# Turning the attention weights on VectorE and through memory, and one batch of weighted sums per pair of tiles

## The chip, the cores and the metric

The kernel runs on one core of a Trainium2 chip. A core has a matrix engine (TensorE, in the profile PE for its products and PEld for loading the stationary operand), a vector engine (VectorE, DVE), a scalar engine (ScalarE, ACT), GpSimd (POOL), and a queue engine (SyncE, SP) that issues transfers. Transfers are carried by 16 DMA engines. The on-chip memory SBUF has 128 partitions; products land in PSUM, which has eight banks of 128 x 512 fp32 values. The metric is the time of one execution on the device in microseconds (us), the median of several runs.

## The reference

Two layers over `x` of 128 graphs x 64 nodes x 768 features, with one adjacency matrix per graph. The first is a graph network with relation embeddings (pass 1 of the kernel), the second an attention layer with six heads of 128 features (pass 2). The change is in the second:

```
hh   = relu(layernorm(x))
h    = einsum('bni,hio->bhno', hh, W)              # six heads
th   = tanh(h);  attn = th@w_src + (th@w_dst)^T     # 64 x 64 per graph and head
attn = softmax(where(adj == 0, -999, leaky(attn)))
f    = elu(einsum('bhnm,bhmo->bhno', attn, h) + b)
gate = sigmoid(hh @ H_w.T + H_b)
out  = x + gate * f + (1 - gate) * hh
```

Everything is fp32.

## The kernel before

A tile is two graphs: 128 rows. There are 64 tiles in 32 pairs. Pass 1 (up to 1425 us) computes the first layer and leaves, per pair, three things in device memory: `x`, half of `hh`, and `hh` turned (`H1D`). Pass 2 reads them back pair by pair.

In pass 2 the products `hh @ [W | H_w]` of a pair are computed in a scheme with 15 products of thirds instead of 18 (`PRODUCTS`). Names in the written order are steps: `F<name>` forms a sum of operand blocks on VectorE (`form`); `P<k>.<q>` is one half of product k on TensorE (`half_product`, L1050); `R<k>` adds a product's bank to its place on VectorE (`read`, L1077, L1079), `RA<k>` the part that ScalarE copies where a place is begun (`read_act`, L1066). Products accumulate in four kinds of banks: `pma` (two buffers), `pmb`, `pmc`, `pmd` (one each), five of the eight banks. The other three are `ps`, taken in turn by everything else.

For each tile t of the pair (0 or 1) the attention follows: `th` tanh; `mul` multiply by the two vectors; `sum` row sums by ScalarE; `k`, `chain` small GpSimd work; `swap` a copy of the heads with the graphs exchanged (`hx`, two SP transfers, L1121); `rows`, `log` two small products; `rrow`, `lrow` their copies; `cp` the mask; `pre` leaky; `tr` row maxima; `exp` the exponentials into `pb` with their sums in `dn`; `rec` one over the sums. Then the weights are turned: `turnp` has three 128x128 transposes on TensorE into one `ps` bank (L1185), `pT` a ScalarE copy to SBUF (L1190). `att` computes the weighted sums (L1203): 12 products per tile, each with a stationary operand of 64 rows and 64 columns, so that four fit on the array side by side; the two row halves go to two `ps` banks. `ev` scales three heads by `dn` and adds the bias (L1213, VectorE), `e` exponentiates, `f` three final steps (L1231, L1233, L1235), `g` the gate, and `dma` adds the result to the output by a GpSimd transfer (L1238).

The order of all this is written out by hand as two strings. `ORDER` is one iteration of a loop over pairs; `name/k` means that the step is done for the pair k iterations back. `END` follows the loop and holds everything that is then left. Each engine executes its own instructions strictly in the order of these strings, except SP in pass 2, whose transfers are ordered by the planner; there the loads of the next pair are issued at an iteration's start. Six positions of iteration 0 (`j in (33, 56, ...)`) finish the last two tiles of pass 1. The queue's `load_h` (L369) fetches a pair's turned `hh` in eight transfers with pieces of 128 bytes.

Of the kernel before, what the change touches and what calls it, by code (L numbers as in the profile page):

```python
# [101 lines left out]


ORDER = """
R8/1 P7.0/1 f1.1/3 tr0/2 P9.0/1 P7.1/1 RA7/1 chain1/2 R7/1 P9.1/1 P11.1/1 f0.2/3 rows1/2 P10.0/1
R9/1 rrow1/2 exp0.0/2 P2.0 lrow1/2 P10.1/1 exp0.1/2 log1/2 P12.0/1 Ff1 turnp0/2 P12.1/1 f1.2/3
P0.0 R11/1 R10/1 th0/1 P13.0/1 P2.1 Ff8 cp1/2 mul0/1 Ff2 dma1/3 R12/1 Ff5 pre1/2 pT0/2 P0.1 Ff3
sum0.1/1 Ff7 P14.0/1 sum0.0/1 RA0 P13.1/1 memset0/1 Ff9 P14.1/1 R2 att0/2 sum0.2/1 tr1/2 Ff4
rec0/2 P5.0 R0 R13/1 dma0/3 Ff6 sum0.3/1 RA14/1 R14/1 exp1.0/2 ev0.1/2 k0/1 P3.0 chain0/1 Ff10
P1.0 exp1.1/2 th1/1 P3.1 ev0.0/2 turnp1/2 RA2 Ff11 e0/2 P1.1 P8.0 mul1/1 RA1 R1 P5.1 g1/1 pT1/2  # L110
rows0/1 R3 P4.0 lrow0/1 P6.0 f0.0/2 g0/1 att1/2 sum1.2/1 rec1/2 rrow0/1 f0.1/2 sum1.0/1 sum1.3/1
RA5 ev1.1/2 log0/1 swap1/1 sum1.1/1 swap0/1 P6.1 R5 ev1.0/2 e1/2 P4.1 P8.1 k1/1 R4 cp0/1 pre0/1
memset1/1 R6 P11.0 f1.0/2
""".split()

END = """
tr0/3 f0.2/4 R8/2 P7.0/2 P9.0/2 f1.1/4 P7.1/2 exp0.0/3 exp0.1/3 RA7/2 chain1/3 P9.1/2 memset0/2
P11.1/2 R7/2 rec0/3 R9/2 rows1/3 P10.0/2 Ff1/1 R11/2 th0/2 f1.2/4 turnp0/3 Ff2/1 P0.0/1 rrow1/3  # L120
P10.1/2 P12.0/2 pT0/3 lrow1/3 Ff3/1 log1/3 R10/2 dma0/4 Ff7/1 P0.1/1 g0/2 mul0/2 cp1/3 Ff8/1
P2.0/1 att0/3 P13.0/2 sum0.1/2 dma1/4 sum0.2/2 Ff4/1 R0/1 Ff5/1 P12.1/2 P13.1/2 Ff9/1 P2.1/1
RA0/1 sum0.0/2 ev0.1/3 ev0.0/3 P3.0/1 pre1/3 R13/2 sum0.3/2 tr1/3 Ff6/1 k0/2 P1.0/1 e0/3
exp1.0/3 chain0/2 P3.1/1 R12/2 P1.1/1 f0.0/3 RA1/1 rows0/2 P14.0/2 R2/1 RA2/1 R1/1 Ff10/1
rrow0/2 lrow0/2 P4.0/1 P14.1/2 exp1.1/3 log0/2 f0.1/3 R3/1 P5.0/1 Ff1 R14/2 f0.2/3 P6.0/1 cp0/2
P4.1/1 RA14/2 Ff11/1 turnp1/3 P6.1/1 th1/2 rec1/3 mul1/2 P5.1/1 pre0/2 pT1/3 R4/1 sum1.3/2
sum1.0/2 RA5/1 tr0/2 att1/3 P7.0/1 R5/1 Ff2 P8.0/1 ev1.1/3 P7.1/1 sum1.1/2 sum1.2/2 R6/1 Ff8
swap0/2 P9.0/1 k1/2 exp0.0/2 P11.0/1 Ff7 ev1.0/3 P9.1/1 chain1/2 swap1/2 g1/2 Ff5 P8.1/1 R7/1
P11.1/1 RA7/1 exp0.1/2 e1/3 Ff3 Ff4 rows1/2 P10.0/1 Ff6 R9/1 R8/1 R11/1 Ff9 lrow1/2 P12.0/1
th0/1 turnp0/2 rrow1/2 rec0/2 memset1/2 P10.1/1 f1.0/3 pT0/2 mul0/1 R10/1 PH2 sum0.3/1 log1/2  # L130
dma0/3 Ff10 P12.1/1 PH0 P13.0/1 R12/1 RAH2 sum0.0/1 P14.0/1 P13.1/1 att0/2 f1.1/3 sum0.2/1 cp1/2
pre1/2 f1.2/3 P14.1/1 tr1/2 sum0.1/1 R13/1 RAH0 ev0.0/2 PH3 PH1 exp1.0/2 PH5 R14/1 memset0/1
k0/1 ev0.1/2 chain0/1 rows0/1 RH3 Ff11 RA14/1 th1/1 e0/2 PH8 RAH1 exp1.1/2 mul1/1 PH4 rrow0/1
PH6 f0.0/2 swap0/1 lrow0/1 rec1/2 turnp1/2 sum1.1/1 sum1.0/1 sum1.3/1 RH4 pT1/2 memset1/1 log0/1
dma1/3 PH7 RH6 f0.1/2 cp0/1 RAH5 PH9 f0.2/2 PH11 RAH7 pre0/1 att1/2 RH9 g1/1 tr0/1 RH8 k1/1 PG0
RH11 sum1.2/1 ev1.0/2 PG5 g0/1 PH10 ev1.1/2 th0 chain1/1 PH12 RG0 mul0 RH10 rows1/1 rrow1/1
exp0.0/1 dma0/2 e1/2 PH13 exp0.1/1 sum0.1 f1.0/2 RH12 PG3 PG2 lrow1/1 log1/1 sum0.0 RH13 swap1/1
f1.1/2 sum0.2 PH14 rec0/1 PG1 RG2 sum0.3 cp1/1 turnp0/1 RG3 RAH14 pre1/1 f1.2/2 th1 RG1 tr1/1
PG6 k0 pT0/1 chain0 mul1 exp1.0/1 exp1.1/1 PG4 dma1/2 rows0 rrow0 RG4 att0/1 PG8 lrow0 ev0.0/1
turnp1/1 memset0 ev0.1/1 sum1.0 log0 PG7 memset1 pT1/1 RG6 rec1/1 e0/1 att1/1 sum1.2 RG5 PG9 cp0  # L140
sum1.1 sum1.3 pre0 f0.0/1 PG11 RG7 f0.1/1 k1 ev1.0/1 ev1.1/1 tr0 RG9 e1/1 chain1 exp0.0 rows1
f0.2/1 RG11 lrow1 rrow1 log1 swap1 exp0.1 f1.0/1 PG10 RG8 cp1 pre1 f1.1/1 tr1 turnp0 swap0 rec0
pT0 exp1.0 f1.2/1 att0 exp1.1 RG10 PG12 dma0/1 ev0.0 ev0.1 e0.0 rec1 RG12 f0.0.0 PG13 RG13
f0.1.0 e0.1 turnp1 PG14 g0 f0.0.1 RG14 f0.1.1 dma1/1 pT1 f0.2.0 att1 ev1.1 ev1.0 out0.0 f0.2.1
e1.1 f1.0.1 e1.0 g1 f1.0.0 f1.1.1 f1.1.0 f1.2.1 f1.2.0 out0.1 f1.3.1 f1.3.0 out1.1 out1.0
""".split()


# [1 line left out]
def kernel(  # L150
# [819 lines left out]
    with ExitStack() as px:  # L970
# [221 lines left out]
        def attend(t):


            hs = hz(t)[0]
            po = PO[t] = [pss.tile([P, 512], F32, name="ps")[:, : HH * DO].rearrange(
                "p (c o) -> p c o", c=HH) for r in range(2)]
            for c in range(HH):
                for g in range(GT):
                    for r in range(2):  # L1200
                        s = slice(r * N, (r + 1) * N)
                        o = slice(g * N, (g + 1) * N)
                        nc.tensor.matmul(po[r][o, c, :], PT[t][s, c, o],  # L1203
                                         (hs if r == g else HX[t])[s, 2 * c + r, :],
                                         start=True, stop=True)
# [206 lines left out]
```

## Time and profile before

| | us |
|---|---|
| median of 3 runs (lowest, highest) | 2384.75 (2384.31, 2386.83) |
| profiled execution | 2385.08 |
| its span | 2383.3 |
| pass 1 | to about 1425 |
| one period of pass 2 (one pair) | 29.18 |

| group of pass 2 | count | busy us |
|---|---|---|
| transposes of the weights, PE L1185 | 192 | 31.4 |
| copy of the turned weights, ACT L1190 | 64 | 30.4 |
| weighted sums, PE L1203 | 1536 | 112.7 |
| scaling of the sums, DVE L1213 | 384 | 110.1 |

The profile's busy times overlap on PE, since matmuls are pipelined: a group's sum is more than what it adds to the span. How far one instruction pushes the next is read from the distance between starts. A fp32 matmul appears as two records. Stretches of time are counted from the span's start.

### The profile page before, as it was taken

Reading aid. Unit: us, or ns where it says so; the run is one execution under the profiler, and the core shown is the slowest. Engines: PE = TensorE matmul, PEld = TensorE weight load, DVE = VectorE, ACT = ScalarE, POOL = GpSimd, SP = SyncE. Lnnn points to the kernel's source line nnn. Section 1 sums busy time; section 2 is a strip of 40 time slices with the busy share of each in tenths; the row PEclk is TensorE's granted clock in tenths of the full one; section 3 lists DMA queues with packets and bytes.
Section 4 is the critical chain, followed back from the end, with each engine's and each line's share of the span. In section 5 each row is a group of like instructions: output and inputs, shape, how many; then the busy total and the mean of one; then the engine's idle time right before and its main releaser. Section 6 shows DMA issues by size and latency. Waiting matters only on the chain.

```text
span 2383.3 us, 35466 instructions
## 1 busy us (share of the span) xinstructions
PE 2359.6 (99%) x11777; PEld 1660.7 (70%) x11777; DVE 1954.0 (82%) x3611; ACT 1339.6 (56%) x4017; POOL 381.6 (16%) x983
## 2 busy tenths in 40 slices
PE   9999999999999999999999999999999999999997
PEld 7888888888888888888888884444444444444445
DVE  8878787787787787877877876888888888888899
ACT  3454454544544544545545425677777777777777
POOL 1111111111111111111111111111111111111122
PEclk9999999999999999999999999999999999999999
DMA  5235335335344353353353466665555555555545
GB/s 186 83 89 139 101 94 151 90 98 142 89 117 123 89 136 104 92 151 92 96 143 89 108 187 125 117 113 109 109 110 114 115 113 110 109 109 114 114 94 100
DMA packets 582906, 271.80 MB, mean 114 GB/s; under 512 B 424394, under 2 KB 533053, under 8 KB 582722
## 3 DMA queue, kind: packets, MB, share of 16 engines
q1 hardware_dynamic: 572850, 244.71, 40.9%
q0 software_dynamic: 9728, 24.78, 7.0%
q8 instruction: 93, 1.52, 0.3%
q14 instruction: 91, 0.75, 0.1%
q10 hardware_dynamic: 144, 0.04, 0.0%
HBM read 119.66 MB, written 124.26 MB: 102 GB/s over the span
## 4 chain that ended last, share of the span: by engine, by line
PE 93%; DVE 3%; ACT 1%; DMA 1%; issue 0%; SPq 0%; POOL 0%; DVEq 0%; POOLq 0%; ACTq 0%
PE pwa L745 20%; PE pwb L745 17%; PE pwcd L745 13%; PE pma L1050 13%; PE pmb L1050 11%; PE pmc L1050 5%; PE pmd L1050 4%; PE pb L673 2%; PE ps L1203 2%; PE pwcd L729 1%; PE pwcd L673 1%; PE ps L1185 1%; ACT pr L1102 1%; PE ps L1154 1%; DVE weights L344 1%
## 5 line engine op out<-in xcount | busy, mean ns | idle before, releaser
L745 PE MATMUL pwa<-weights,op 128*128 128x256 f32 x2304 | 539.4, 381 | 0.3 <-DVE x L737 0.3
L745 PEld LDWEIGHTS pwa<-weights,op 128*128 128x128 f32 x2304 | 422.3, 190 | 53.8 <-issue 1.1
L745 PE MATMUL pwb<-weights,op 128*128 128x256 f32 x1932 | 454.5, 381 | 0.0
L745 PEld LDWEIGHTS pwb<-weights,op 128*128 128x128 f32 x1932 | 359.4, 190 | 53.1 <-issue 0.2
L344 DVE TENSOR_TENSOR op<-op 128x768 f32<-128x768 f32 x310 | 291.5, 949 | 95.6 <-ACT op L683 91.7
L745 PE MATMUL pwcd<-weights,op 128*128 128x256 f32 x1560 | 357.8, 379 | 0.0
L745 PEld LDWEIGHTS pwcd<-weights,op 128*128 128x128 f32 x1560 | 296.1, 190 | 40.1
L1050 PE MATMUL pma<-weights,op_f 128*128 128x512 f32 x620 | 310.3, 597 | 2.6 <-ACT hh L783 2.2
L683 ACT COPY op<-pb 128x512 f32<-128x512 f32 (+1 forms) x132 | 70.8, 618 | 320.5 <-PE pb L673 320.4
L1102 ACT ACTIVATE pr<-pr 128x128 f32<-128x128 f32 x768 | 225.3, 296 | 25.1 <-DVE pr L1092 25.0
L1050 PEld LDWEIGHTS pma<-weights,op_f 128*128 128x128 f32 x620 | 112.2, 190 | 140.4 <-issue 103.2
L1050 PE MATMUL pmb<-weights,op_f 128*128 128x512 f32 x372 | 193.1, 601 | 0.4 <-DVE hz L1077 0.4
L321 POOL TENSOR_SCALAR rn<-su 128x1 f32<-128x1 f32 x124 | 28.0, 226 | 902.0 <-ACT hf L316 531.1
L531 ACT ACTIVATE hp<-x,rn 128x768 f32<-128x768 f32 x60 | 107.7, 1796 | 109.8 <-POOL rn L323 109.8
L315 ACT ACTIVATE hf<-x 128x768 f32<-128x768 f32 x64 | 53.5, 836 | 163.6 <-DVE x L781 150.1
L1102 ACT ACTIVATION_READ_ACCUMULATOR pr<-pr 128x1 f32 x768 | 144.4, 188 | 0.0
L1175 ACT ACTIVATE pb<-al,mx 128x64 f32<-128x64 f32 x384 | 128.5, 338 | 12.3 <-DVE mx L1167 11.6
L1050 PE MATMUL pmc<-weights,op_f 128*128 128x512 f32 x248 | 129.7, 604 | 0.2 <-DVE weights L1079 0.2
L1213 DVE SCALAR_TENSOR_TENSOR f<-ps,dn,bb 128x128 f32<-128x128 f32 x384 | 110.1, 343 | 21.9 <-PE ps L1203 20.3
L1050 PE MATMUL pmb<-weights,h 128*128 128x512 f32 x248 | 127.7, 596 | 0.0
L737 DVE TENSOR_TENSOR x<-pwa,x 128x256 f32<-128x256 f32 x96 | 40.5, 422 | 100.0 <-PE pwa L729 72.1
L624 DVE TENSOR_REDUCE sum<-eq 128x26 f32<-128x1664 bf16 x64 | 120.0, 1875 | 0.1
...
## 6 DMA issues: line engine op xcount, KB each, us to landing
...
```

What stands on the lines that cost most here:

```text
L315: nc.scalar.activation(by, src, AF.Copy, scale=-1.0 / D, accum_out=sums[:, 0:1])
L344: return (nc.vector.tensor_add if s1 == "+" else nc.vector.tensor_sub)(to, x, y)
L531: nc.scalar.activation(hp.rearrange("p (b f i) -> p b f i", b=KB, f=NQ), X[t].rearrange("p (b i f) -> p b f i", b=KB, f=NQ), AF.Relu, scal ...
L624: nc.vector.tensor_reduce(SUM[p][:, k], EQ[p, k], AX.X, OP.add)
L673: nc.tensor.matmul(to[:, g, :, i, :], H0[2 * p + k][o, kb * P : (kb + 1) * P], rts[p % 2][o, k, :n].rearrange("p s n -> p (s n)"), start=T ...
L683: nc.scalar.copy(a[:, :n].rearrange("p s h (g n) -> p g (s h) n", g=GT), ps[:, :, c * n * KQ * N : (c + 1) * n * KQ * N].rearrange("p g (x ...
L745: nc.tensor.matmul(bank[b][:, :CQ], OPS[p, an][:, s, q, :], bw[bn][:, (s * KQ + q) * CQ : (s * KQ + q + 1) * CQ], start=(first and q == s ...
L1050: nc.tensor.matmul(bank[p, b], operand(p, an)[:, q, :], bw2[bn][:, 2 * q * CQ : 2 * (q + 1) * CQ], start=(first and q == 0), stop=(q == KQ ...
L1102: nc.scalar.activation(PR[t][:, j, h, :], PR[t][:, j, h, :], AF.Copy, accum_out=to)
L1175: nc.scalar.activation(PB[t][:, h, :], AL[t][:, h, :], AF.Exp, bias=MX[t][:, h : h + 1], accum_out=DN[t][:, h : h + 1])
L1203: nc.tensor.matmul(po[r][o, c, :], PT[t][s, c, o], (hs if r == g else HX[t])[s, 2 * c + r, :], start=True, stop=True)
L1213: nc.vector.scalar_tensor_tensor(FF[t][:, h * DO : (h + 1) * DO], PO[t][r][:, c, :], DN[t][:, h : h + 1], bb, op0=OP.mult, op1=OP.add)
```

## The change

- `turn_blocks` (`tv`): one VectorE transpose per tile that turns each 32x32 block of the 128x384 weights where it lies. `put_blocks` (`ts`): four SP transfers per tile write the blocks to device memory, in pieces of 128 bytes, each to where it belongs in the turned matrix. `get_blocks` (`tl`): one SP transfer reads the turned matrix back, in pieces of 512 bytes. They replace `turnp` and `pT` for all pairs but the last.
- `attend_both` (`att` without a tile number): the weighted sums of both tiles in one batch of 24 products over two `ps` banks and the banks `pmc` and `pmd`. In a bank each row half stays by itself. For the second last and the last pair `attend` per tile stays, for the last also `turnp` and `pT`.
- The load of `hh` for the final steps is a step of its own (`lx`), and so is the load of the next pair (`ld`). SP executes in written order too.
- `ORDER` and `END` are new throughout. Per tile, the steps `att`, `ev`, `e`, `f` are now up to four iterations behind. `FINISH` has the last two tiles of pass 1 finished in iterations 1 and 2.

```diff
+FINISH = (158, 189, 215, 216, 242, 268)
...
+    PTD = [dram.tile([KB // 2 * P, P], F32, name=f"pt_{t}") for t in range(NT)]
...
+        def turn_blocks(t):
+            TP[t] = work.tile([P, H * N], F32, name="tp")
+            nc.vector.transpose(TP[t], PB[t].rearrange("p h n -> p (h n)"))
+
+        def put_blocks(t):
+            for f in range(NQ):
+                nc.sync.dma_start(
+                    PTD[t].rearrange("(x i) (f n) -> f i x n", i=Q, n=Q)[f],
+                    TP[t][f * Q : (f + 1) * Q].rearrange("i (x n) -> i x n", n=Q))
+
+        def get_blocks(t):
+            PT[t] = work.tile([P, HH, P], F32, name="pT")
+            nc.sync.dma_start(PT[t], PTD[t].rearrange("(c p) n -> p c n", p=P))
+
+        def weigh(t, c, r):
+            hs = hz(t)[0]
+            s = slice(r * N, (r + 1) * N)
+            for g in range(GT):
+                o = slice(g * N, (g + 1) * N)
+                nc.tensor.matmul(PO[t][r][c][o, :], PT[t][s, c, o],
+                                 (hs if r == g else HX[t])[s, 2 * c + r, :],
+                                 start=True, stop=True)
...
+        def attend_both(p):
+            t = 2 * p
+            a, b, c, d = places(2, "cd")
+            PO[t] = a[:3], b[:3]
+            PO[t + 1] = (a[3], c[0], c[1]), (b[3], d[0], d[1])
+            for k in range(2):
+                for i in range(HH):
+                    weigh(t + k, i, 0)
+                    weigh(t + 1 - k, i, 1)
...
+            if n == "att":
+                attend_both(p)
+            elif n == "ld":
+                load(p + 1)
...
-        px.enter_context(tc.manual_schedule(engines=in_order))
+        px.enter_context(tc.manual_schedule(engines=in_order | {mybir.EngineType.SP}))
...
-            if i >= 0:
-                load(i + 1)
             for j, (n, k) in enumerate(order):
-                if i == 0 and j in (33, 56, 62, 78, 100, 106):
+                if i * len(order) + j in FINISH:
```

The new loop iteration, in which `att` is one batch:

```
dma0/4 R1/1 RA1/1 P3.1/1 R2/1 memset1/2 R14/2 th1/2 R3/1 tv1/3 P11.0/1 rows0/2 P4.0/1 rrow0/2
lrow0/2 tl0/3 mul1/2 P6.0/1 Ff1 P4.1/1 R4/1 Ff6/1 log0/2 P6.1/1 P11.1/1 sum1.2/2 R6/1 sum1.3/2
sum1.0/2 Ff7 sum1.1/2 P7.0/1 k1/2 cp0/2 Ff4 lx1/3 P7.1/1 rec0/3 Ff2 P9.0/1 Ff8 Ff11/1 R7/1 P9.1/1
pre0/2 RA7/1 tr0/2 chain1/2 P8.0/1 Ff9 P8.1/1 R9/1 lx0/3 rows1/2 Ff10 memset0/1 ld R11/1 g1/3
exp0.0/2 ts1/3 rrow1/2 R8/1 P10.0/1 P10.1/1 exp0.1/2 Ff3 swap0/3 lrow1/2 th0/1 P12.0/1 tv0/2 R10/1
P12.1/1 mul0/1 tl1/3 g0/2 att/3 log1/2 R12/1 ev1.0/3 ev1.1/3 cp1/2 sum0.3/1 ev0.0/3 sum0.1/1 P13.0/1
e1/3 f1.0/3 P13.1/1 P14.0/1 sum0.0/1 P14.1/1 P2.0 P2.1 R13/1 ev0.1/3 P1.0 pre1/2 f1.1/3 sum0.2/1
tr1/2 f1.2/3 P0.0 P0.1 e0/3 dma1/3 P5.0 f0.0/3 swap1/2 P5.1 exp1.0/2 RA0 R0 P1.1 exp1.1/2 f0.1/3
ts0/2 RA5 k0/1 chain0/1 rec1/2 Ff5 RA14/1 P3.0 f0.2/3 R5 RA2
```

More of the change, by code (lines that the diff above doesn't have):

```diff
@@ L104 @@
 ORDER = """
[L105 to L110, printed above, removed]
@@ L111 @@
-rows0/1 R3 P4.0 lrow0/1 P6.0 f0.0/2 g0/1 att1/2 sum1.2/1 rec1/2 rrow0/1 f0.1/2 sum1.0/1 sum1.3/1
-RA5 ev1.1/2 log0/1 swap1/1 sum1.1/1 swap0/1 P6.1 R5 ev1.0/2 e1/2 P4.1 P8.1 k1/1 R4 cp0/1 pre0/1
-memset1/1 R6 P11.0 f1.0/2
+dma0/4 R1/1 RA1/1 P3.1/1 R2/1 memset1/2 R14/2 th1/2 R3/1 tv1/3 P11.0/1 rows0/2 P4.0/1 rrow0/2
+lrow0/2 tl0/3 mul1/2 P6.0/1 Ff1 P4.1/1 R4/1 Ff6/1 log0/2 P6.1/1 P11.1/1 sum1.2/2 R6/1 sum1.3/2
+sum1.0/2 Ff7 sum1.1/2 P7.0/1 k1/2 cp0/2 Ff4 lx1/3 P7.1/1 rec0/3 Ff2 P9.0/1 Ff8 Ff11/1 R7/1 P9.1/1
@@ L114 @@
 """.split()
+FINISH = (158, 189, 215, 216, 242, 268)
 END = """
[L119 to L145, printed above, removed]
+Ff6/2 rows0/3 R1/2 P3.1/2 RA1/2 lrow0/3 tv1/4 Ff1/1 rrow0/3 R2/2 R14/3 P11.0/2 th1/3 P4.0/2
+memset1/3 R3/2 log0/3 ts1/4 tl1/4 Ff5/1 Ff11/2 mul1/3 P4.1/2 P6.0/2 P6.1/2 sum1.2/3 sum1.3/3 R4/2
@@ new lines @@
+lx1/4 P8.0/2 swap0/4 Ff7/1 sum1.0/3 P8.1/2 R6/2 sum1.1/3 P7.0/2 Ff2/1 k1/3 R8/2 P7.1/2 dma0/5 P9.0/2
+g1/4 Ff8/1 P9.1/2 cp0/3 Ff9/1 R7/2 Ff4/1 pre0/3 Ff3/1 P11.1/2 Ff10/1 RA7/2 lx0/4 tr0/3 R9/2 Ff6/1
+P10.0/2 chain1/3 rows1/3 R11/2 tl0/4 rrow1/3 th0/2 Ff11/1 P10.1/2 R10/2 g1/3 mul0/2 att/4 rec0/4
+lrow1/3 ev1.0/4 log1/3 ld/1 exp0.0/3 sum0.0/2 ev1.1/4 P13.0/2 P13.1/2 P12.0/2 sum0.1/2 ev0.1/4 cp1/3
+ev0.0/4 e1/4 R13/2 P12.1/2 exp0.1/3 P2.0/1 e0/4 k0/2 P2.1/1 f1.0/4 sum0.2/2 sum0.3/2 chain0/2 P0.0/1
@@ new lines @@
+R12/2 P0.1/1 f1.1/4 f0.0/4 f1.2/4 P1.0/1 f0.1/4 R0/1 tv0/3 P1.1/1 dma1/4 pre1/3 P5.0/1 g0/3 f0.2/4
+rows0/2 P14.0/2 P14.1/2 RA0/1 RA1/1 rec0/3 tr1/3 R2/1 R1/1 RA14/2 P3.0/1 lx1/3 P3.1/1 P5.1/1 P4.0/1
+R14/2 RA2/1 th1/2 R3/1 P4.1/1 memset0/2 exp1.0/3 rrow0/2 lrow0/2 P6.0/1 ts0/3 log0/2 mul1/2 P6.1/1
+exp1.1/3 swap1/3 R5/1 Ff1 P8.0/1 tv1/3 R4/1 Ff2 sum1.1/2 P7.0/1 cp0/2 R6/1 RA5/1 P7.1/1 sum1.0/2
+sum1.3/2 sum1.2/2 k1/2 P9.0/1 Ff5 Ff7 Ff8 Ff4 P9.1/1 RA7/1 rec1/3 pre0/2 P11.0/1 chain1/2 ts1/3 Ff9
@@ new lines @@
+swap0/3 tl0/3 lx0/3 tl1/3 Ff3 memset1/2 rows1/2 tr0/2 R7/1 dma0/4 Ff10 P11.1/1 lrow1/2 R9/1 P8.1/1
+Ff6 exp0.0/2 rrow1/2 R11/1 exp0.1/2 R8/1 th0/1 Ff11 log1/2 P10.0/1 cp1/2 P10.1/1 tv0/2 att/3 mul0/1
+pre1/2 sum0.0/1 R10/1 tr1/2 sum0.1/1 P12.0/1 P12.1/1 memset1/1 sum0.2/1 ev0.1/3 ev0.0/3 ev1.0/3 e0/3
+PG0 P13.0/1 swap1/2 ev1.1/3 memset0/1 g0/2 PH5 P13.1/1 f0.0/3 e1/3 R12/1 f0.1/3 exp1.0/2 PH2 R13/1
+f0.2/3 sum0.3/1 dma0/3 exp1.1/2 RAH2 f1.0/3 P14.0/1 g1/2 ts0/2 P14.1/1 R14/1 PH1 RA14/1 tv1/2 k0/1
@@ new lines @@
+tl0/2 RAH1 PH8 chain0/1 PH0 th1/1 f1.1/3 rows0/1 swap0/2 f1.2/3 PH4 mul1/1 RAH0 PH3 lx0/2 RAH5
+lrow0/1 sum1.1/1 sum1.0/1 sum1.3/1 PH11 RH3 ts1/2 PH6 lx0/1 rec1/2 rrow0/1 RH4 log0/1 RH6 PH7 k1/1
+RAH7 RG0 cp0/1 RH8 PH9 rec0/2 PH10 sum1.2/1 RH9 pre0/1 dma1/3 RH11 RH10 tr0/1 th0 PH12 exp0.0/1
+tl1/2 lx1/2 chain1/1 rows1/1 exp0.1/1 RH12 mul0 rrow1/1 sum0.2 tv0/1 att/2 sum0.0 ev1.1/2 PG3 sum0.1
+lrow1/1 PH13 PH14 ev0.1/2 ev0.0/2 RH13 log1/1 PG2 e0/2 ev1.0/2 RAH14 sum0.3 cp1/1 ts0/1 k0 pre1/1
+chain0 PG1 f0.0/2 rec0/1 e1/2 f0.1/2 rows0 memset0 RG2 th1 tr1/1 f0.2/2 exp1.0/1 mul1 exp1.1/1
@@ new lines @@
+swap0/1 g1/1 dma0/2 tv1/1 tl0/1 lrow0 RG1 RG3 ts1/1 rrow0 PG4 log0 PG6 sum1.2 sum1.0 att0/1 sum1.1
+f1.0/2 RG4 swap1/1 k1 sum1.3 f1.1/2 PG7 cp0 f1.2/2 chain1 ev0.0/1 tl1/1 ev0.1/1 RG7 rec1/1 pre0 tr0
+RG6 dma1/2 rows1 e0/1 PG5 f0.0/1 PG10 rrow1 g0/1 f0.1/1 exp0.0 lrow1 att1/1 PG9 swap1 RG5 log1
+memset1 f0.2/1 exp0.1 ev1.1/1 ev1.0/1 turnp0 PG8 RG10 cp1 lx1/1 e1/1 swap0 RG9 PG12 f1.0/1 pre1 tr1
+pT0 att0 exp1.0 f1.1/1 rec0 f1.2/1 dma0/1 PG11 lx0 RG12 ev0.1 dma1/1 ev0.0 PG13 RG8 PG14 exp1.1 RG13
@@ L146 @@
+e0.0 RG11 e0.1 f0.0.0 f0.0.1 rec1 lx1 RG14 f0.1.1 g0 turnp1 pT1 f0.1.0 g1 att1 f0.2.1 ev1.0 e1.0
+out0.1 ev1.1 f1.0.0 f1.1.0 e1.1 f1.0.1 f1.2.0 f1.1.1 f1.3.0 f1.2.1 f1.3.1 out1.0 f0.2.0 out0.0
+out1.1
 """.split()
@@ L1082, in hz @@
             return (hzs[t % NHZ][:, 0, :].rearrange("p (h o) -> p h o", h=H), hzs[t % NHZ][:, 1, :])
-        TH, PR, SD, SG, PS, AM, AL, PB, DN, MX, PT, PO, FF, EE, HX = ({} for _ in range(15))
+        TH, PR, SD, SG, PS, AM, AL, PB, DN, MX, PT, PO, FF, EE, HX, TP = ({} for _ in range(16))
         def tanh(t):
@@ new lines, in weigh, with places @@
+        def weigh(t, c, r):
[6 more added lines that the diff above has]
+                                 start=True, stop=True)
+        def places(n, more=""):
+            banks = [pss.tile([P, 512], F32, name="ps") for _ in range(n)]
+            banks += [psm.tile([P, 512], F32, name=f"pm{b}", bufs=1) for b in more]
+            return [[v[:, i * DO : (i + 1) * DO] for i in range(512 // DO)] for v in banks]
@@ L1192, in attend @@
         def attend(t):
-            hs = hz(t)[0]
-            po = PO[t] = [pss.tile([P, 512], F32, name="ps")[:, : HH * DO].rearrange(
-                "p (c o) -> p c o", c=HH) for r in range(2)]
+            PO[t] = places(2)
             for c in range(HH):
[L1199 to L1205, printed above, removed]
+                for r in range(2):
+                    weigh(t, c, r)
@@ L1213, in divide @@
                 nc.vector.scalar_tensor_tensor(
-                    FF[t][:, h * DO : (h + 1) * DO], PO[t][r][:, c, :], DN[t][:, h : h + 1], bb,
+                    FF[t][:, h * DO : (h + 1) * DO], PO[t][r][c], DN[t][:, h : h + 1], bb,
                     op0=OP.mult, op1=OP.add)
@@ L1242 @@
             "rrow": rows_dst, "lrow": rows_src, "memset": fill,
-            "log": lambda t: (load_x(t), logits(t)), "cp": choose, "pre": leaky, "tr": largest,
-            "rec": one_over, "turnp": turn_p, "pT": copy_p, "att": attend, "g": gate, "e": exp_f,
+            "lx": load_x, "log": logits, "cp": choose, "pre": leaky, "tr": largest,
+            "rec": one_over, "tv": turn_blocks, "ts": put_blocks, "tl": get_blocks, "turnp": turn_p, "pT": copy_p,
+            "att": attend, "g": gate, "e": exp_f,
             "dma": store,
@@ L1249, in step @@
         def step(n, p):
-            if n[0] == "F":
+            if n == "att":
+                attend_both(p)
+            elif n == "ld":
+                load(p + 1)
+            elif n[0] == "F":
                 form(p, n[1:])
@@ L1337, in last_step @@
                 step(n, p)
-                if n[:-1] == "log":
+                if n[:-1] == "lx":
                     load_out(2 * p + int(n[-1]))
@@ L1360 @@
                     step(n, i - k)
-        load(NP - 1)
         for n, k in parsed(END):
```

## The prediction, made before the changed kernel was run

> **What bounds the kernel now.** I read the engine totals first, then the busy time by stretch, then the chain of work that ended last, and last PE's order in time inside one period of pass 2. The totals:
>
> ```profile
> PE 2359.6 (99%) x11777; PEld 1660.7 (70%) x11777; DVE 1954.0 (82%) x3611; ACT 1339.6 (56%) x4017; POOL 381.6 (16%) x983
> ```
>
> PE is busy for all but 24 us. The stretches say where it is not (columns: stretch, length, busy time of PE, PEld, DVE, ACT, POOL, granted clock, DMA share, GB/s):
>
> ```profile
> 1429.00:1450.00 21.00, 18.76 (x44) 8.08 (x43) 11.27 (x20) 8.31 (x14) 2.26 (x10) 1.00 1.00 207
> ...
> 1878.28:1907.46 29.18, 29.18 (x119) 13.14 (x118) 26.19 (x55) 20.82 (x91) 5.11 (x17) 1.00 0.58 110
> ...
> 2286.80:2383.30 96.50, 81.28 (x457) 48.47 (x455) 88.15 (x191) 68.42 (x299) 21.37 (x55) 0.95 0.47 94
> ```
>
> The middle row is one period of pass 2: a pair of tiles each 29.18 us, PE without a gap, DVE idle for 3.0 us. The chain repeats at that distance 27 times (1478.27 to 2266.09 us). The last row is all that END writes out: there PE idles for 15 us and DVE for 8.35, so **END is set by VectorE**, the loop by PE. The chain in pass 2 agrees: its lines are the half products L1050 (80%), then L1203 (4.7%) and L1185 (1.9%).
>
> PE inside that period, start and length:
>
> ```profile
> 1885.42 1.02 PE L1050 MATMUL pma<-weights,op_f 128*128 128x512 f32 x2
> 1886.28 0.49 PE L1185 MATMUL ps<-ident,pb 128*128 128x128 f32 x3
> 1886.60 1.88 PE L1050 MATMUL pma<-weights,op_f 128*128 128x512 f32 x4
> ...
> 1892.62 1.02 PE L1050 MATMUL pma<-weights,op_f 128*128 128x512 f32 x2
> 1893.57 0.32 PE L1203 MATMUL ps<-hz,pT 64*64 64x128 f32 x1
> 1893.57 0.33 PE L1203 MATMUL ps<-hx,pT 64*64 64x128 f32 x2
> ...
> 1894.18 0.27 PE L1203 MATMUL ps<-hz,pT 64*64 64x128 f32 x1
> 1894.38 1.12 PE L1050 MATMUL pmc<-weights,op_f 128*128 128x512 f32 x2
> 1895.35 1.02 PE L1050 MATMUL pma<-weights,op_f 128*128 128x512 f32 x2
> ```
>
> Lengths overlap, so I price by start-to-start distance. A half product (two records) is 1886.28 - 1885.42 = 0.86, 0.858 over longer runs. Three transposes take 1886.60 - 1886.28 = 0.325. One tile's weighted sums take 1895.35 - 1892.62 - 2 x 0.858 = 1.01, the other tile's (ahead of a logit product) 0.91. Rows cost 0.083, logits 0.172. A period: 30 x 0.858 + 2 x (0.325 + 0.083 + 0.172) + 1.92 = 28.82. Most of the remaining 0.36 is P7 and P9 held up for VectorE's reads R4 and R6.
>
> **PE's part of the change.** The transposes go: -0.65 a pair. In the weighted sums four 64x64 quadrants start together, and then four every 0.107 us. Around a batch there are 0.10 us before it, 0.05 for the slower first step, and 0.10 + 0.11 before the wide products are back in step. Twelve steps in one batch cost 0.36 + 12 x 0.107 = 1.64 in place of 1.92: -0.28. The new period's work is 27.89.
>
> **VectorE's part.** One 32x32-block transpose of 128x384 is added per tile. The nearest row is pass 1's, the same instruction in f32 on twice the width:
>
> ```profile
> L793 DVE STREAM_TRANSPOSE ht<-hf x64: 916/969/978, 92.4 to 1439.6; 128x768 f32<-128x768 f32 x64
> ```
>
> Half is 0.49 us; two make DVE's period 26.19 + 0.98 = 27.17, against PE's 27.89. A rule speaks against this move: the Trainium skill, "VectorE: DVE Perf Modes", section "The three transpose paths", prices VectorE at 311 ns for 128x128 (bf16), and its rules for authors say to turn 128x128 on TensorE if PSUM will do. Three squares at that price are 0.93 a tile; DVE's period would be 28.05, and VectorE would set the loop. The row has the kernel's own type and form, so I take 0.49 and keep 0.93 for the range.
>
> **ScalarE** loses two copies of pT (L1190, 475 ns each). It is busy for 20.82 of 29.18; its share of the gain is nothing, since it sets no end in the loop.
>
> **New waits.** Writing each engine's steps of the new ORDER one after another with such distances (VectorE: form or half read 0.34, full read 0.60, multiply 1.66, final step 0.87, three divides 0.78, the 384-wide ones 0.43 to 0.48; stretched by 2%, as 25.68 before stood for 26.19 measured), PE reaches att at 14.9 and ends it at 16.5; its results are there at about 16.75. VectorE reaches ev1.0 at 16.0, so it waits there 0.75, and behind it stand ev1.1, cp1, ev0.0 and then e1 on ScalarE. That uses up its margin of 0.72 in one place. What PE needs from VectorE is then still early: R3 done at 1.8 for P6 at 2.7, R4 at 5.3 for P7 at 6.3, f11 at 8.6 for P8 at 9.7. Banks c and d, which att borrows, are read (R11, R8) by 12.3, and ev1.1 frees them at 18.3 for P2 at 20.1. So paper gives no stall; I take 0.25 a period (nothing to 0.7), since margins of one us are met by an in-order VectorE with 0.7 to spare.
>
> **SP and the queues.** Per pair SP now issues 8 puts of 48 KB and 2 gets of 192 KB more: 25 transfers in place of 15, at 0.3 to 0.55 each some 11 of 27.9 us. SP is in written order now: swap1 waits for att, ts0 stands behind it, tl0 waits for ts0's landing, and behind tl0 stand both x loads and all of the next pair's loads (needed 20 us later). The tight one is tile 1: tv1 ends at 2.1, its four puts are issued by 4.0, then swap0 (5.1), then tl1. In pass 1 such a put and reload is visible:
>
> ```profile
> 1273.75 0.36 SPq L542 DMA_DIRECT2D h<-hpt  x1
> 1276.33 0.36 SPq L556 DMA_DIRECT2D op<-h  x1
> ```
>
> 2.6 us from put to reload. The load of the next pair (6,144 packets of 128 B) lies ahead. Over ten periods 71,230 packets took 39.8% of 16 engines over 291.8 us, 26 ns each, so it drains in at most 10 us and, begun near -4, by about 5; puts until 8, landed 9, tl1 landed 12; att wants it at 14.9. Three us are left. The puts add 3,072 packets of 128 B and the gets 768 of 512 B a pair: at 26 ns, 6.2 us of the 16 engines. DMA goes from 0.58 x 29.18 = 17.0 to 23.2 us of 28.1, a share of 0.83.
> The Trainium skill, "DMA: Bandwidth & Descriptors", Specifications, speaks against the puts: under 512 B a transfer is a read-modify-write. The row is for reads in 128 B pieces; 128 B writes to DRAM are not in this trace. Nothing is lost up to (28.1 - 17.0 - 1.2) x 16 / 3,072 = 51 ns a packet; there the queue is full. By the row the sum is the forecast; past 51 ns it is the third rival.
>
> **The sum.** Pass 2 before: iteration 0 holds 17 half products (14.6), iteration 1 26.0, 28 periods of 29.18 are 817.0, and PE's waits at its beginning 2.9 (L1050 for ScalarE L783, 2.2): 860.5, from 1426.0 to END at 2286.8. The new order runs a longer pipeline: iteration 0 holds 9 half products (7.7), iteration 1 25.7, iteration 2 26.3, then 27 periods of 28.14 are 759.8; beginning 1.5, because the last tiles of pass 1 are finished an iteration later: 821.0. **END therefore gets longer.** By the distances above its list held 85.0 us of VectorE before (88.15 measured, x1.037) and holds 100.2 now: 103.9, and with the same 8.35 idle 112.3 in place of 96.5. Span: 1426.0 + 821.0 + 112.3 = 2359.3, against 2383.3. The profiled execution took 2385.08, 1.8 more than its span, and the median is 2384.75; so 2361. Of 40 us that the loop gives, END takes 16 back. END from 106 (better order) to 119, stalls from 0 to 0.7: 2348 to 2379, with both ends at once unlikely: 2350 to 2373.
>
> **Rivals.** (1) PE's rate holds, as above: chance 0.65, including a luckier end down to 2345. (2) *VectorE becomes the loop's bound*: 28.05 by the page's price plus 0.3 of waits; 27 x 28.35 = 765.5, END +3.4: about 2370; up to 2380 with more waits. For it: only 0.7 of margin, against 3.0 before. Chance 0.18. (3) *The reload is late*, at att, on PE: a wait takes the place of the transposes. The gain is used up when tl1 lands more than 24/27 = 0.9 us past 14.9 in every period beyond my 0.25; two us late give 2361 + 54 = 2415, one us 2388. Three us of margin and a DMA share under 0.9 are against it. Chance 0.08. (4) *The batch doesn't do what it says*: the new order issues both quadrants of one row half before the other's; if only two run together, 24 steps of 0.107 make it 2.93, the period 29.4, and the time 2361 + 27 x 1.29 + 4 = 2400. That the trace starts all four within 0.02 us speaks against it. Chance 0.04. The rest, 0.05, is stalls that nearly cancel the gain.
>
> A measurement tells about 0.2% (5 us) from no change. Faster: (1), (2) and 0.03 of the near-cancelling stalls, 0.86. Same: their other 0.02 and the mildest 0.02 of (3), 0.04. Slower: the rest of (3), and (4), 0.10. For 8 in 10 I go from 2345 to 2378.
>
> **What would show it.** Marks of the period 28.0 to 28.3 apart; no L1185 in the loop; one batch of 48 matmul records of about 1.5 us; L1205 at 0.5 us; DVE 96% busy in the loop; END near 2247, about 112 long, VectorE over 90% busy. Wrong if PE waits at the sums for a DMA, if DVE is at 100%, or if END isn't longer.

## The result, and the profile after

The changed kernel takes 2364.59 us (median of 4 runs, 2362.86 to 2365.44), the kernel before on the same chip 2385.52 (4 runs). The ratio is 0.9911, 95% interval 0.9894 to 0.9928: 0.9% faster. The forecast of 2361 is 3.6 us too low. The profiled execution took 2364.23 us with a span of 2362.4.

Line numbers have moved: the half products (L1050 before) are L1059, the weighted sums L1224, the scaling of the sums L1260, the three final steps L1278, L1280 and L1282, split L1122 and L1124, SP's `h` loads L378.

The engine totals of the changed kernel's page:

```profile
PE 2326.6 (98%) x11591; PEld 1654.4 (70%) x11591; DVE 1979.1 (84%) x3673; ACT 1303.9 (55%) x3955; POOL 441.4 (19%) x983
```

PE has 33 us less, VectorE 25 more, and GpSimd 60 us more with the same 983 instructions. That last number was in no step of the forecast; the part of it that falls in END (32.2 us where END had 21.4 before) bears on what the forecast missed.

The busy time by stretch (stretch, length, busy PE, PEld, DVE, ACT, POOL, granted clock, DMA share, GB/s): one period, what END writes out, and the loop ahead of it.

```profile
1753.62:1781.50 27.88, 27.88 (x113) 12.83 (x113) 26.99 (x57) 19.64 (x90) 6.75 (x16) 1.00 0.71 145
2238.74:2362.40 123.66, 93.44 (x506) 55.13 (x505) 101.81 (x222) 75.30 (x325) 32.17 (x60) 0.87 0.61 130
1426.00:2238.74 812.74, 812.74 (x3166) 372.80 (x3167) 768.40 (x1590) 562.40 (x2507) 198.92 (x474) 1.00 0.70 141
```

A period is 27.88 us where it was 29.18. VectorE is busy for 97% of it, and PE still has no gap. The loop ends 8.3 us earlier than forecast (812.7 us, not 821.0). END is 11.4 us longer than forecast (123.7, not 112.3), and PE works at a mean clock of 0.87 there. So the total was close because two errors cancel, and in part by luck: a loop that was better than I said, and an END that was worse.

The loop has no transposes of the weights on PE left: the six that remain (L1194) are those of the last pair, in END. The batch begins like this in time (start, length, instruction); the four quadrants start within 0.03 us of each other, and a new set follows every 0.11 us:

```profile
1751.81 0.32 PE L1224 MATMUL ps<-weights,pT 64*64 64x128 f32 x1
1751.81 0.33 PE L1224 MATMUL ps<-hx,pT 64*64 64x128 f32 x2
1751.83 0.41 PE L1224 MATMUL ps<-weights,pT 64*64 64x128 f32 x2
...
1753.28 0.34 PE L1163 MATMUL ps<-rrow,lrow 82*128 82x384 bf16 x1
```

From the batch's first start to the logit product behind it are 1.47 us. The VectorE transposes as a group (shortest, median and longest ns, first and last start, shape):

```profile
L1205 DVE STREAM_TRANSPOSE tp<-pb x62: 560/564/575, 1472.6 to 2321.2; 128x384 f32<-128x384 f32 x62
```

Lengths overlap: behind the one that starts at 2264.08 the next instruction starts at 2264.58, 0.50 us later (forecast 0.49).

**END.** VectorE did less work there than forecast (101.8, not 103.9) but idled for 21.9 us, not 8.35. Of that, 7.4 us lie behind its last instruction, and the longest gaps before instructions are these (in brackets the idle time ahead, and who ended it):

```profile
2270.05 0.42 DVE L1086 TENSOR_TENSOR hz<-pma,weights 128x256 f32<-128x256 f32 x1 [3.38 <-ACT hz L1075]
2303.85 0.42 DVE L1339 TENSOR_TENSOR weights<-weights,pma 128x256 f32<-128x256 f32 x1 [4.07 <-PE pma L1322]
2343.40 1.64 DVE L1260 SCALAR_TENSOR_TENSOR f<-ps,dn,bb 128x128 f32<-128x128 f32 x6 [2.93 <-DMA out_dram<-f]
```

The first one can be followed back. PE, in time:

```profile
2262.43 1.02 PE L1059 MATMUL pmc<-weights,op_f 128*128 128x512 f32 x2
2265.89 0.38 PE L1144 MATMUL ps<-idr,sdb 128*82 128x192 bf16 x1 [2.44 <-POOL sdb L1122]
2266.07 5.25 PE L1059 MATMUL pma<-weights,op_f 128*128 128x512 f32 x8
```

PE waits 2.44 us for `rows`, that is for GpSimd's small `chain` (split, L1122 and L1124). Eight half-bank records then take 5.1 us from start to start, where they take 3.4 elsewhere: after the wait the granted clock was 0.52 for 3.4 us, by the busy times of that stretch:

```profile
2265.80:2269.20 3.40, 3.31 (x5) 1.58 (x6) 0.87 (x3) 0.00 (x0) 1.35 (x3) 0.52 0.82 105
```

The Trainium skill, "TensorE: Matmul & The Clock Gate", Part 1, says that TensorE falls back to 4 of 8 clock pulses after an idle window of about 3.4 us and is released after about 3.4 us of busy time. The 0.52 and the 3.4 us of this stretch fit; the wait was shorter than that window, and a second execution (below) had the same wait without the slow clock. In this execution the wait of 2.44 us thus cost some 1.6 us more. GpSimd's instructions in that time:

```profile
2261.14 2.75 POOL L1122 CAST sdb<-sg 128x18 bf16<-128x18 f32 x1 [4.23 <-issue]
...
2264.25 0.20 POOL L1122 CAST sdb<-sg 128x18 bf16<-128x18 f32 x1
2264.53 1.05 POOL L1124 TENSOR_TENSOR sg<-sg,sdb 128x18 f32<-128x18 f32 x1
```

VectorE's, in the same time:

```profile
2261.14 0.95 DVE L1278 SCALAR_TENSOR_TENSOR f<-e,f 128x768 f32<-128x768 f32 x1
2262.01 0.94 DVE L1282 SCALAR_TENSOR_TENSOR f<-weights,f 128x768 f32<-128x768 f32 x1
2262.88 0.95 DVE L1280 SCALAR_TENSOR_TENSOR f<-f,x 128x768 f32<-128x768 f32 x1
2263.75 0.41 DVE L1086 TENSOR_TENSOR weights<-pma,weights 128x256 f32<-128x256 f32 x1
```

A cast of 18 columns takes 0.20 us, or 2.75 us where VectorE runs three final steps in a row, whose operands are all in SBUF; it ends when VectorE goes on to an operand in PSUM. It starts right behind ScalarE's last sum for this tile, which ends at 2261.0. The chain of work that ended last runs through it (start, length, what; "issue" is time for which the profile shows no cause):

```profile
2256.91 4.22 issue
2261.14 2.76 POOL sdb L1122
2264.53 1.05 POOL sg L1124
...
2266.28 5.04 PE pma L1059 x8
```

Added up over END, split's two lines take 11.2 us of that chain, and 1.1 us of the chain in END before. Some 38 of its 118 us are "issue", so the chain alone doesn't settle what holds END.

### The profile page after: what moved, and what is told of

The parts are those of the page before. It is cut to its first block, busy times and chain, and to the rows that moved or that the text cites. A ratio compares the mean times of both kernels' runs of the same rounds, so it can differ in the third digit from the quotient of the medians.

```text
span 2362.4 us, 35548 instructions
## 1 busy us (share of the span) xinstructions
PE 2326.6 (98%) x11591; PEld 1654.4 (70%) x11591; DVE 1979.1 (84%) x3673; ACT 1303.9 (55%) x3955; POOL 441.4 (19%) x983
## 4 chain that ended last, share of the span: by engine, by line
PE 93%; DVE 3%; issue 2%; DMA 1%; POOL 1%; ACT 0%; SPq 0%; POOLq 0%; DVEq 0%
PE pwa L754 21%; PE pwb L754 17%; PE pwcd L754 14%; PE pma L1059 13%; PE pmb L1059 11%; PE pmd L1059 4%; PE pmc L1059 4%; PE pb L682 3%; PE ps L1224 1%; PE pwcd L738 1%; PE pwcd L682 1%; PE ps L1163 1%; DVE weights L353 1%; PE pmc L1224 0%; PE pwa L738 0%
## 5 line engine op out<-in xcount | busy, mean ns | idle before, releaser
L1059 PE MATMUL pma<-weights,op_f 128*128 128x512 f32 x620 | 293.1, 595 | 0.0
L1059 PEld LDWEIGHTS pma<-weights,op_f 128*128 128x128 f32 x620 | 118.2, 191 | 147.6 <-issue 139.2
L1059 PE MATMUL pmb<-weights,op_f 128*128 128x512 f32 x372 | 180.7, 594 | 0.0
L1285 POOL DMA_DIRECT2D out_dram<-f x62 | 55.0, 886 | 390.1 <-DVE f L1282 376.8
L1059 PEld LDWEIGHTS pmb<-weights,op_f 128*128 128x128 f32 x372 | 68.4, 190 | 83.7 <-issue 76.0
L1059 PE MATMUL pmb<-weights,h 128*128 128x512 f32 x248 | 122.5, 595 | 0.0
L1059 PE MATMUL pmc<-weights,op_f 128*128 128x512 f32 x248 | 121.8, 592 | 0.0
```

Source lines behind the costliest of these rows:

```text
L1059: nc.tensor.matmul(bank[p, b], operand(p, an)[:, q, :], bw2[bn][:, 2 * q * CQ : 2 * (q + 1) * CQ], start=(first and q == 0), stop=(q == KQ ...
L1285: nc.gpsimd.dma_start(of[t * P : (t + 1) * P, :], FF[t], accum_op=OP.add)
```

## The experiments

The theories: (A) in the loop PE's own work sets the time, and the change gains by taking work off PE; in END PE waits for GpSimd's chain, and VectorE waits for PE. (B), the prediction's: END is set by the amount of VectorE's work. Rivals for the loop: VectorE at 97% is as good as the bound; the reload is close to the path.

### One part undone at a time

*split_batch* cuts the batch in two, each part with one row half of either tile, and puts the logit product between them; *turn_on_pe* puts the three TensorE transposes and ScalarE's copy back, and keeps the batch; *both_back* does both. The new order is kept in all three.

```diff
-P12.1/1 mul0/1 tl1/3 g0/2 att/3 log1/2 R12/1 ...
+P12.1/1 mul0/1 tl1/3 g0/2 atA/3 log1/2 atB/3 R12/1 ...
```

```diff
-dma0/4 R1/1 RA1/1 P3.1/1 ... R3/1 tv1/3 P11.0/1 rows0/2 P4.0/1 rrow0/2
-lrow0/2 tl0/3 mul1/2 P6.0/1 ...          (and no ts, tl, tv elsewhere)
+dma0/4 R1/1 RA1/1 P3.1/1 ... R3/1 turnp1/3 P11.0/1 pT1/3 rows0/2 P4.0/1 rrow0/2
+lrow0/2 turnp0/3 mul1/2 pT0/3 P6.0/1 ...
```

> In the loop the batch of weighted sums is cut in two, with the logit product of the other tile between the halves; nothing else changes (END keeps its batches). If the entry and exit of a batch cost PE what was read off the trace before (0.28 us a period), the period goes from 27.88 to about 28.16 us and the time to 2364.6 + 27 x 0.28 = 2372. If the batching is worth nothing, because VectorE or a transfer sets the period, the period stays at 27.9 and the time at 2365. If the cut leaves a stall behind ev1.0, more than 28.3 and above 2376.

> The changed kernel's order, with the weights turned by three TensorE transposes and a ScalarE copy again in place of the VectorE transpose, the puts and the reload; the batch stays. If PE sets the loop, the period grows by two times three transposes, 0.65 us, to 28.53, and the time is 2364.6 + 27 x 0.65 = 2382, less up to 4 us in END, where VectorE has 0.5 us less for each of the last seven tiles: 2378 to 2382. If VectorE or the reload set the loop, taking their work away leaves the period at 27.9 or below, and the time at 2365 or below.

> Both parts undone in the changed order: transposes on TensorE, batch cut in two. If they add up, the period is 27.88 + 0.65 + 0.28 = 28.81 us, the 0.37 left to the 29.18 of before is what the new order saves in stalls, and the time is about 2388: above the kernel before, since END stays longer than before's. If the order alone carries the gain, the time stays near 2365.

Measured (single executions; the kernel before took 2386.7 beside them): 2373.64, 2383.08 and 2393.71 us. The busy times of one period, for split_batch:

```profile
1752.55:1780.79 28.24, 28.24 (x114) 12.85 (x113) 27.17 (x57) 19.64 (x88) 6.73 (x16) 1.00 0.69 137
```

for turn_on_pe:

```profile
1755.39:1783.94 28.55, 28.55 (x119) 13.41 (x119) 26.39 (x55) 20.50 (x91) 6.96 (x16) 1.00 0.56 114
```

and for both_back:

```profile
1758.53:1787.43 28.90, 28.90 (x120) 13.41 (x119) 26.50 (x55) 20.50 (x91) 6.89 (x16) 1.00 0.58 112
```

Against 27.88 the batch is worth 0.36 us a period, the transposes 0.66, both together 1.01: they add. (The expectations had 0.28, 0.65 and 0.93.) What is left of the 1.30 between before and after, 29.18 - 28.90 = 0.28, belongs to the new order alone, which has both old parts and still stalls less. That order by itself is no gain: both_back is slower than before (2393.7 against 2386.7). Its loop ends 20 us earlier than the old one (at 2266.8), but its END is 125.2 us long where it was 96.5; the 2388 that was expected of it is 6 us too low.

### VectorE loaded to the brim

*turn_twice* does each VectorE transpose twice.

```diff
-            nc.vector.transpose(TP[t], PB[t].rearrange("p h n -> p (h n)"))
+            for _ in range(2):
+                nc.vector.transpose(TP[t], PB[t].rearrange("p h n -> p (h n)"))
```

> Each VectorE transpose of the weights is done twice (same output); nothing else changes. VectorE is busy for 26.98 of 27.88 us in a period; two more transposes bring its work to about 27.98. If PE sets the period with VectorE 0.9 below it, the period goes only to 28.0 to 28.3, and END grows by some 4 us: 2371 to 2380. If VectorE sets the period already, the whole 1.0 us is added: 28.9, and 2395.

Measured (a single execution, beside 2386.7 of the kernel before): 2362.02 us. The busy times of one period and of END:

```profile
1750.00:1777.88 27.88, 27.88 (x114) 12.83 (x113) 27.78 (x59) 19.66 (x89) 6.79 (x16) 1.00 0.71 144
2239.60:2360.20 120.60, 90.24 (x505) 52.93 (x505) 105.62 (x229) 75.31 (x325) 29.70 (x62) 0.91 0.63 134
```

VectorE is busy for 99.6% of a period and the period doesn't move, not even by the 0.1 to 0.4 us that my own theory expected, whose 2371 to 2380 us were wrong too. END has 3.8 us more VectorE work and is 3 us shorter (1 us, against the second execution below). Both the rival for the loop and theory B fall here: VectorE's work in END isn't what sets its length.

### The puts doubled

*puts_twice* issues each of a pair's eight puts twice, to the same place.

```diff
-            for f in range(NQ):
+            for f in (*range(NQ), *range(NQ)):
```

> Each of the eight puts of a pair (48 KB in pieces of 128 B) is issued twice, to the same place; the result is the same. 3,072 more packets of 128 B a pair: at 26 ns each the DMA share goes from 0.71 to about 0.89, and SP issues for about 27 of 27.9 us in place of 22.6. Theory: the transfers are off the path by 2 to 5 us, so a period that stays at 27.9 - 28.0 for the most part means that neither queue nor SP was near setting the loop (2364 to 2368). The rival of the late reload: the reload comes later by the four to eight added issues, 2 to 4 us, PE waits at the weighted sums in each period, and the period is 28.5 to 30 (2380 to 2420). A write of 128 B that costs the queues 51 ns or more would show as a DMA share of 1.0 with such a period.

Measured (a single execution, beside 2387.4 of the kernel before): 2440.38 us, 76 more. My theory's numbers for this run were wrong. The rival's mechanism is right, and even its 28.5 to 30 us a period and 2380 to 2420 us were too low. The busy times of one period, from one `swap1` to the next:

```profile
2025.86:2056.24 30.38, 28.99 (x115) 13.52 (x112) 27.18 (x57) 19.65 (x88) 6.99 (x16) 0.99 0.76 146
```

SP's issues in it (start, length, transfers in a row):

```profile
2025.86 1.10 SPq L1130 DMA_DIRECT2D hx<-weights  x2
2027.01 4.44 SPq L1210 DMA_DIRECT2D pt<-tp  x8
2032.87 0.38 SPq L1216 DMA_DIRECT2D pT<-pt  x1
...
2034.31 10.82 SPq L378 DMA_DIRECT2D h<-h  x8
...
2045.80 4.45 SPq L1210 DMA_DIRECT2D pt<-tp  x8
...
2051.71 0.39 SPq L1216 DMA_DIRECT2D pT<-pt  x1
2056.24 1.10 SPq L1130 DMA_DIRECT2D hx<-weights  x2
```

PE, at the weighted sums of that period:

```profile
2054.56 0.32 PE L1224 MATMUL ps<-hx,pT 64*64 64x128 f32 x1 [1.02 <-DMA pT<-pt]
```

The DMA share is 0.76, so the queues have room: 0.76 x 30.38 = 23.1 us against 19.8 in the changed kernel, 17 ns for each of the 3,072 writes added. What closes is a ring: `swap1` waits for `att`; behind it, in SP's order, stand tile 0's puts and reload, the next pair's loads, tile 1's puts and reload; and `att` waits for that reload. The same ring in the changed kernel, by SP's issues:

```profile
1753.41 1.10 SPq L1130 DMA_DIRECT2D hx<-weights  x2
1754.56 2.29 SPq L1210 DMA_DIRECT2D pt<-tp  x4
...
1760.63 10.76 SPq L378 DMA_DIRECT2D h<-h  x8
...
1772.06 1.97 SPq L1210 DMA_DIRECT2D pt<-tp  x4
...
1775.46 0.39 SPq L1216 DMA_DIRECT2D pT<-pt  x1
```

The reload is issued at 1775.46; in puts_twice one lands 2054.56 - 2051.71 = 2.85 us after its issue, which would be 1778.3; `att` begins at 1779.69. That leaves 1.4 us; in the period before it (issued 1746.74, `att` at 1751.81) it leaves 2.2. Eight more puts add 4.44 + 4.45 - 2.29 - 1.97 = 4.6 us to the ring, and this period is longer by 2.5: the difference, 2.1, is the slack. So the changed kernel's loop is free of the reload by 1.4 to 2.2 us and no more.

### What holds END

*chain_free* moves two ScalarE sums and one store in END, so that GpSimd's chain may begin earlier and stands behind no store. *chain_on_vector* gives the chain's five steps to VectorE for the last seven tiles. *tail* sums and stores the second last tile in parts, as the last one is, and begins its last parts earlier.

```diff
-... P12.0/2 sum0.1/2 ev0.1/4 cp1/3 ev0.0/4 e1/4 ... e0/4 k0/2 P2.1/1 f1.0/4 sum0.2/2 sum0.3/2 chain0/2
+... P12.0/2 sum0.1/2 sum0.2/2 sum0.3/2 ev0.1/4 cp1/3 ev0.0/4 e1/4 ... e0/4 k0/2 P2.1/1 f1.0/4 chain0/2
...
-f0.2/3 sum0.3/1 dma0/3 exp1.1/2 ... PH8 chain0/1 PH0
+f0.2/3 sum0.3/1 exp1.1/2 ... PH8 chain0/1 dma0/3 PH0
```

```diff
+            e = nc.vector if t >= NT - 7 else nc.gpsimd
-                nc.gpsimd.tensor_copy(q, SG[t])
+                e.tensor_copy(q, SG[t])
-                    nc.gpsimd.tensor_sub(SG[t], SG[t], q)
+                    e.tensor_sub(SG[t], SG[t], q)
```

```diff
-... f0.2.1 ev1.0 e1.0 out0.1 ev1.1 f1.0.0 f1.1.0 e1.1 f1.0.1 ... f1.3.1 out1.0 f0.2.0 out0.0 out1.1
+... f0.2.1 f0.3.1 ev1.0 e1.0 out0.1 ev1.1 f1.0.0 f1.1.0 e1.1 f0.2.0 f0.3.0 out0.0 f1.0.1 ... f1.3.1 out1.0 out1.1
...
-        SUMMED_HERE = (NT - 1,)
+        SUMMED_HERE = (NT - 2, NT - 1)
```

> END only, two steps moved: sum0.2/2 and sum0.3/2 stand directly behind sum0.1/2 on ScalarE's list (so chain0/2 on GpSimd may begin some 2.5 us earlier), and the store dma0/3 stands behind chain0/1 on GpSimd's list, not ahead of it. Nothing is computed differently. Theory A, that END is held by PE waiting for rows, which waits for GpSimd's chain: the 2.4 us wait of PE at 2263.4 to 2265.9 goes, and some of the 4 us that VectorE waits for PE near 2300; END from 123.7 to 118 - 121, so 2359 to 2362 us. Theory B (the prediction's), that END is set by VectorE's own amount of work, 101.8 us: END stays within 0.7 us, 2364 to 2365.

> The five small steps of split (three casts, two subtractions, 128x18) run on VectorE in place of GpSimd for the last seven tiles, that is in END only. Same numbers come out. VectorE gets 35 more instructions there, at 0.1 to 0.2 us some 3.5 to 7 us of work. Theory A (GpSimd's chain, slowed to 1 - 2.7 us an instruction while VectorE works between SBUF tiles, holds PE's rows): PE's waits for sdb fall below half of what they were, and END gets shorter or stays in spite of the added VectorE work: 2360 to 2365. Theory B (VectorE's amount of work sets END): END grows by the added work, 2368 to 2372. Between the two, VectorE now waiting in order for ScalarE's sums ahead of each chain would give 2365 to 2368.

> Only the end of END: tile NT-2 is also summed and stored in parts, as tile NT-1 is, and its last parts f0.2, f0.3, out0.0 stand ahead of f1.0.1. The last store then follows the last VectorE step by one part and not by a whole tile. VectorE's last step stood 7.4 us ahead of the span's end, against 4.1 before the change. Theory: this tail is part of what END lost, about 3 us: 7.4 falls to 4 - 5 us, 2361 to 2363 us. If the tail is the fixed price of a last store whatever stands ahead: 2364 to 2366.

Measured (single executions; the kernel before took 2387.4 beside them): 2358.38, 2363.26 and 2362.45 us. The busy times of END in chain_free:

```profile
2240.44:2356.60 116.16, 89.92 (x506) 53.25 (x505) 101.71 (x222) 75.22 (x325) 29.65 (x60) 0.89 0.66 139
```

in chain_on_vector:

```profile
2238.82:2361.50 122.68, 90.58 (x506) 53.74 (x505) 106.99 (x257) 75.21 (x325) 15.02 (x25) 0.88 0.63 131
```

and in tail:

```profile
2239.76:2360.70 120.94, 93.61 (x506) 55.13 (x505) 102.82 (x224) 75.31 (x325) 29.80 (x58) 0.88 0.62 137
```

chain_free makes END 7.5 us shorter than the profiled 123.7 with the same VectorE work (101.7), a little more than was expected. Its chain for tile 0 of that pair is done 21.8 us after END's start, 27.1 in the changed kernel: it starts 2.6 us earlier (19.8 against 22.4) and takes 2.7 us less (2.0 against 4.7). GpSimd's instructions:

```profile
2260.20 0.20 POOL L1122 CAST sdb<-sg 128x18 bf16<-128x18 f32 x1 [1.59 <-issue]
...
2262.04 0.20 POOL L1122 CAST sdb<-sg 128x18 bf16<-128x18 f32 x1
```

It now runs ahead of the run of final steps and not beside it; one subtraction still falls beside a single final step and takes 0.93. The gaps of 3.38 and 4.07 us on VectorE are gone (the second is 0.51), and so is the half clock behind the first: 1.00 where it was 0.52. What each of the two moves gives by itself was not measured. chain_on_vector adds 5.2 us of VectorE work and END gets 1.0 shorter, where theory B has it 5.2 longer. PE's waits for the chain fall from 8.6 us to 3.2 in all; one of 5.7 us for VectorE (L1340) is new, which may be why END gains no more. tail has 3.4 us behind VectorE's last instruction where there were 7.4, and END is 2.7 shorter.

How steady is END itself? The changed kernel, run again with the next experiment, had an END of 121.75 us in its profiled execution, and a gap of 1.69 in place of the 3.38. PE's wait, and the stretch from there:

```profile
2268.51 0.28 PE L1144 MATMUL ps<-idr,sdb 128*82 128x192 bf16 x1 [2.44 <-POOL sdb L1122]
2268.40:2271.80 3.40, 3.29 (x9) 1.62 (x10) 1.32 (x4) 1.23 (x3) 1.37 (x3) 1.00 0.81 95
```

The wait is the same to 0.01 us, but the clock stays at 1.00: the slow clock behind it comes in some executions and not in others, and it explains some 1.6 of the 1.9 us between the two ENDs. Differences of under 2 us in END, chain_on_vector's own gain among them, are within that; chain_free's 5.6 to 7.5 are not. tail's execution had the slow clock too (its eight half-bank records take 5.3 us), so its 2.7 is rightly counted from the first.

### Three edits of END together

*three_in_end* is chain_free, tail, and a third buffer for the tiles `f`, which takes away the wait of 2.93 us for a store:

```diff
-            TP[t] = work.tile([P, H * N], F32, name="tp")
+            TP[t] = work.tile([P, H * N], F32, name="tp", bufs=1)
...
-                FF[t] = work.tile([P, D], F32, name="f")
+                FF[t] = work.tile([P, D], F32, name="f", bufs=3)
```

> END only, three edits at once: the two moved steps of chain_free, the parts of tail, and a third buffer for the tiles f (its room taken from the turned weights tp, which get one buffer in place of two), which is to take away VectorE's wait of 2.9 us for a store to read f. If the three waits are separate, their gains add: 6 us (chain_free as measured), 2 to 2.7 (tail as measured), 2 to 3 (the buffer): 2353 to 2356 us. If they stand behind one another, so that one wait takes the place of the other, 2357 to 2360. The loop is untouched: a period of 27.88 us, unless the single buffer of tp makes VectorE wait for the puts, which would show as a longer period.

> The changed kernel itself, beside three_in_end on the same chip, as the mark that it is compared with: 2362 to 2366 us, END 123 to 124 us long.

Measured on one chip: three_in_end 2351.39 us (4 runs, 2349.81 to 2352.00), the changed kernel 2363.92 (4 runs, 2362.85 to 2364.88), the kernel before 2385.49 (7 runs). The ratios to before are 0.9858 (0.9842 to 0.9875) and 0.9910 (0.9895 to 0.9925). 12.5 us went, somewhat more than the 9 to 12 that were expected if the three gains add: no wait took the place of another. VectorE's wait for a store to read `f` is gone, and PE's longest wait in END, 5.3 us for the last pair's turned weights, is 2.3. The third buffer was not measured alone. The busy times of its END:

```profile
2238.93:2348.00 109.07, 88.43 (x506) 52.23 (x505) 102.57 (x224) 75.28 (x325) 27.33 (x58) 0.94 0.68 151
```

The period is 27.88 as it was. VectorE is now busy for 94% of END, which is 3 us shorter than the 112.3 of the prediction. That VectorE sets this END is still not shown: in the chain that ended last PE has 57 us and VectorE 27.

## Why the prediction was right or wrong

- **The bound of the loop** (PE): right. A period has no gap on PE, and VectorE at 99.6% in turn_twice moves nothing.
- **The transposes, 0.65 a pair**: right, 0.66 by turn_on_pe.
- **The batch, 0.28 a pair**: the mechanism was right, the term too small: one batch more costs 0.36 in split_batch. That is as much as the forecast's sum gives to the edges of one batch (before, first step, behind); as the difference 1.92 - 1.64 it came out too low.
- **Stalls, 0.25 a period**: wrong. Paper gave none, and I put 0.25 there on the ground that an in-order VectorE with 0.7 us to spare must stall PE. Work and stalls together come to 27.88, where 27.89 was forecast for the work alone; the new order, with everything else undone, stands at 28.90, 0.08 over the 28.82 of work, where the old one stood 0.36 over. Over 27 periods this is 7.0 of the 8.3 us by which the loop beat its forecast. The other 1.3, in the loop's beginning, I have not divided further. The wait of 0.75 at `ev1.0` isn't there either: VectorE's longest gaps in the period looked at are 0.44 and 0.34, at other instructions.
- **VectorE's price, 0.49 a transpose and 27.17 a period**: 0.50 from start to start, and 26.99. By busy time two of them add 0.79 in turn_twice, 0.60 to 0.67 between the kernels with and without them. The row of the trace was the better guide. The page's price, with 28.05 a period, would have forbidden the period of 27.88 that was measured.
- **Puts and gets**: the share of 0.83 came out as 0.71. From turn_on_pe to the changed kernel it rises from 0.56 x 28.55 = 16.0 to 0.71 x 27.88 = 19.8 us; for 3,840 packets on 16 engines this is 16 ns each, not 26. The rule on writes under 512 B does not show as a price here: even with the gets at nothing, the 3,072 added writes of 128 bytes come to 20 ns each, and those added in puts_twice to 17, below the 26 of the reads and far below 51.
- **The tight reload, "three us are left"**: wrong by half. All of SP's issues in the period shown in part above take 19.5 us, not some 11 (the rows left out there hold 3.0 of it: a reload, the `x` loads, the mask, `swap0`). The loads of `h` alone take 10.8 for eight, 1.3 us each, where the forecast had 0.3 to 0.55 from the trace of before; and the step missed that SP's written order closes a ring through `att`. The margin is 1.4 to 2.2 us. The rival of the late reload did not come true, but it was nearer than three us: with the puts doubled it is there, at 2440 us.
- **The rival of two quadrants at a time**: refuted by the starts within 0.03 us.
- **END, "set by VectorE", 112.3 us**: this is the step that failed. Its work was well estimated (103.9, measured 101.8), but VectorE is busy for 82% of END, not over 90%. The 8.35 us of idle time was carried over from the old list, though every wait in it was to be new: it is 21.9. The reading behind it was weak already: VectorE's 91% of the old END is a share of busy time, and of the chain that ended last there PE has 29 us, VectorE 26 and ScalarE 24. In its place the runs showed GpSimd's chain starting late and at the same time as VectorE's final steps, PE waiting for `rows` and in one execution working at half clock behind it (5.6 to 7.5 us, chain_free), a last store that follows a whole tile (2.7, tail), and a wait for a buffer of `f` (2.9 in the trace; its part in three_in_end was not measured alone).
- **The total**: 2361 against 2364.6 looks closer than the working was. The loop's 8.3 us too many and END's 11.4 too few cancel for the most part, which is luck.
